# A causal mask moved from TensorE products to a GpSimd select in a gated linear attention layer followed by a quantised MLP

## The chip, the core and the metric

The kernel runs on one core of a Trainium2 chip. TensorE (PE) multiplies matrices and writes its sums to eight PSUM banks; VectorE (DVE), ScalarE (ACT) and GpSimd (POOL) work on tiles in SBUF, the first two on PSUM as well; SyncE (SP) issues nearly all DMAs. Each engine has its own queue and takes its instructions in order; semaphores tie the queues together. The metric is the device time of one execution in microseconds (us), lower is better.

## What is computed

The input x is 4 batches of 512 tokens with 512 features. The first layer is gated linear attention with 4 heads of 128 features over chunks of 128 tokens (4 chunks per batch, 16 in all), the second an MLP whose weights come as four-bit codes with scales.

```python
x = x + attention(layernorm(x))          # y only; the other outputs are dropped
x = x + ffn(layernorm(x))                # NVFP4 weights, 512 -> 4096 (gate, up) -> 512

# attention, per batch b, chunk n, head h
k     = k / max(norm(k), 1e-12)
cla   = cumsum(log(sigmoid(za) + 1e-6))            # within the chunk
decay = where(causal, exp(cla_i - cla_j), 0)       # 128 x 128, lower triangle
attn  = (q @ k.T) * beta_j * decay
y     = attn @ v + (q @ state) * exp(cla_i)
kw    = k * beta * exp(cla_end - cla)
state = state * exp(cla_end) + v.T @ kw
```

The mask `where(causal, ...)` is the part that the change is about.

## The kernel before

**Order of the work.** One schedule is written out by hand (`tc.manual_schedule()`, L811): the order in the code is the order in every queue. A loop over positions p (L856 to L900, then L901) lays a block of TensorE products first and then calls `behind(p)` (L656), which lays the attention work of a chunk behind it. For the first batches a block is `product_v`, `product_q` or `product_k` (four each per batch, L398, L422, L436); near the end of batch 3 the blocks become those of the MLP (`mlp`, L780, with `gate_up` L707 and `down` L745). Chunk (b,n), the chunk n of batch b, takes three positions in a row:

- p % 3 == 0, the lead: `chunk_lead` (L543) transposes k; `take_roots` (L344) runs the square roots of the norms that are waiting; `chunk_decay` (L553) makes the decays.
- p % 3 == 1, the scores: `settle` finishes the norms (among them `brn` and `kwf`, the per-row factors of v and k, L454 to L461, kept in `ss`); `chunk_scores` (L590) makes q·k, kw and vb and multiplies the scores by the decays.
- p % 3 == 2, the sums: `turn` (L358) transposes the normed rows; `chunk_sums` (L615) makes dp (the state's addend) and yp (the output), adds yp to x and starts the second layer's norm.

The factors of a chunk with n = 2 or 3 are usually settled a chunk earlier; those of n = 0 and 1 are settled in the chunk's own scores position. In batch 3, where the k products stand apart, (3,2) is settled in its own scores position too.

**The decays and the mask.** `gates_sums` (L513) makes row sums of the log gates: `rps` (L520) on 48 partitions, of which 0 to 15 hold one row per chunk and head rounded down a little and 32 to 47 the remainder (`pieces`, L521 to L526), and spreads them over the heads' columns (`rowsum`, L527). `all_of` (L159, L178) holds per chunk n a selector, 48 x 128, with ones in the rows of that chunk. In `chunk_decay` the product of selector and rowsum gives every row the cumulative sums of all heads: once as `pc` (L558, only for n > 0), whose exponential `cd` scales q (`qc`, two GpSimd products, L568), and once more as `pm` (L560), onto which a second product (L561) of the identity with `negm` adds -32768 where j > i. Four exponentials (L577), one per head with bias `ncla`, turn pm into `dm`; the -32768 makes the masked entries zero. GpSimd then scales the old state (L585), and in `chunk_scores` makes kw (L607, not for n = 3) and vb (L611). VectorE multiplies dm by the scores (L612).

**GpSimd's queue** for a chunk with n > 0 thus reads qc, qc, state, kw, vb. Without DMAs of its own it holds nothing else but the memset of `la` (L498).

**Buffers.** `Homes` (L94) hands out 42 tiles of 2 KB per partition (`one_k`) and 24 of 4 KB (`two_k`), the longest free first. PSUM tiles go round the eight banks in order.

**Around the change.** The MLP goes over the batches in rounds. The second layer's normed rows are split into three parts, written to HBM (`h<-g`, L388) and read back for each round (`x<-h`, L310); the first MLP round of batch 3 can begin only when (3,3) has been through all of this. Weights are unpacked by VectorE and ScalarE in small steps (`unpack`, L292) between the other work.

Of the kernel before, what the change touches and what calls it, by code (L numbers as in the profile page):

```python
# [21 lines left out]
P = 128  # L22
# [13 lines left out]
def f32(t):  # L36
    return t.bitcast(F32)
# [3 lines left out]
def tile_gated_linear_attention__then__nvfp4_geglu(  # L41
# [90 lines left out]

    ident = const.tile([P, P], F32, tag="ident", name="ident")
    make_identity(nc, ident)
    ident_r = const.tile([P, P], F32R, tag="ident_r", name="ident_r")

    tri = const.tile([P, P], F32, tag="tri", name="tri")
    nc.gpsimd.memset(tri, 1.0)
# [1 line left out]
        out=tri, in_=tri, compare_op=ALU.is_ge, fill=0.0, base=0,  # L140
        pattern=[[1, P]], channel_multiplier=-1,
    )

    home = one_k.get("neg")
    neg = heads(f32(home))
    nc.gpsimd.memset(neg, 0.0)
    nc.gpsimd.affine_select(
        out=neg, in_=neg, compare_op=ALU.is_ge, fill=-32768.0, base=0,
        pattern=[[0, H], [1, P]], channel_multiplier=-1,
    )  # L150
    negm = const.tile([P, H, P], F32R, tag="negm", name="negm")
    ones = const.tile([P, P], F32, tag="ones", name="ones")
    nc.gpsimd.memset(ones, 1.0)


    R2 = 32 + NCH * H
    one_of_h = const.tile([R2, H], F32, tag="one_of_h", name="one_of_h")
    of_n = const.tile([R2, 2, NCH], F32, tag="of_n", name="of_n")
    all_of = const.tile([R2, NCH, P], F32R, tag="all_of", name="all_of")  # L159
    eps_ln = const.tile([P, 1], F32, tag="eps_ln", name="eps_ln")  # L160
    nc.gpsimd.memset(eps_ln, 1e-5)
    eps_la = const.tile([P, 1], F32, tag="eps_la", name="eps_la")
    nc.gpsimd.memset(eps_la, 1e-6)

    def constants():
        nc.vector.tensor_copy(ident_r, ident)
        nc.vector.tensor_copy(negm, neg)
        one_k.put(home)
        nc.vector.tensor_reduce(
            one_of_h, ident[:R2, :R2].rearrange("p (n h) -> p h n", h=H), AX.X, ALU.add  # L170
        )
        for i in range(2):
            nc.vector.tensor_reduce(
                of_n[:, i, :],
                ident[:R2, 32 * i : 32 * i + NCH * H].rearrange("p (n h) -> p n h", h=H), AX.X, ALU.add,
            )
        nc.vector.tensor_tensor(of_n[:, 0, :], of_n[:, 0, :], of_n[:, 1, :], ALU.add)
        nc.vector.tensor_copy(all_of, of_n[:, 0, :].unsqueeze(2).to_broadcast([R2, NCH, P]))  # L178


    def dequant(pk, sc, n, w3, key):
# [306 lines left out]
    def gates_ln(b):  # L488


        ea, u = gt["ea"], gt["u"]
        alpha, w1, dd, eq, lw = (gate(b, nm) for nm in ("alpha", "w1", "dd", "eq", "lw"))
        nc.vector.tensor_scalar(ea, ea, 1.0, None, ALU.add)
        nc.vector.reciprocal(alpha, ea)
        nc.vector.tensor_scalar(w1, u, 1.0, None, ALU.add)

        la = gate(b, "la", R2)
        nc.gpsimd.memset(la, 0.0)  # L498
        nc.scalar.activation(la[:, :NG], alpha, AF.Ln, bias=eps_la)
# [5 lines left out]
        nc.vector.tensor_copy(la[:, 32:], la[:, :NG])  # L505
        nc.vector.tensor_tensor(lw, lw, dd, ALU.mult)
        nc.vector.tensor_tensor(lw, lw, eq, ALU.add)
        nc.vector.tensor_tensor(lw, lw, u, ALU.mult)
        beta[b] = gate(b, "beta")
        zb = zs[b][:, :, H:]  # L510
        nc.vector.scalar_tensor_tensor(th(beta[b]), zb, 0.0, th(lw), ALU.max, ALU.add)

    def gates_sums(b):  # L513
        la = gt["la"]
        cps = psum(f"cps{b}")
        nc.tensor.matmul(cps[:, :NG], tri, la[:, :NG], start=True, stop=True)
        nc.tensor.matmul(cps[:, NG : 2 * NG], ones, la[:, :NG], start=True, stop=True)

        rps = psum(f"rps{b}")
        nc.tensor.matmul(rps[:R2, :P], la, tri, start=True, stop=True)  # L520
        pieces = gate_pool.tile([R2, P], F32R, tag="pieces", name=f"pieces{b}")  # L521
        nc.scalar.activation(pieces, rps[:R2, :P], AF.Copy, scale=HI)
        ncla[b], bdte[b], td[b] = (gate(b, nm) for nm in ("ncla", "bdte", "td"))
        nc.vector.tensor_scalar(ncla[b], cps[:, :NG], -1.0, None, ALU.mult)
        nc.vector.tensor_tensor(bdte[b], cps[:, NG : 2 * NG], ncla[b], ALU.add)
        nc.vector.tensor_tensor(pieces[32:], rps[32:R2, :P], f32(pieces)[32:], ALU.subtract)  # L526
        rowsum[b] = one_k.get(f"rowsum{b}")  # L527
        nc.vector.tensor_tensor(
            heads(rowsum[b][:R2, :]), f32(pieces).unsqueeze(1).to_broadcast([R2, H, P]),
            one_of_h.unsqueeze(2).to_broadcast([R2, H, P]), ALU.mult,  # L530
        )
# [21 lines left out]
    def chunk_decay(b, n):  # L553

        toks = slice(n * P, (n + 1) * P)
        pc = psum(f"pc_{b}_{n}") if n > 0 else None
        if n > 0:
            nc.tensor.matmul(pc, all_of[:, n, :], rowsum[b][:R2, :], start=True, stop=True)  # L558
        pm = psum(f"pm_{b}_{n}")
        nc.tensor.matmul(pm, all_of[:, n, :], rowsum[b][:R2, :], start=True, stop=False)  # L560
        nc.tensor.matmul(pm, ident_r, negm.rearrange("p h c -> p (h c)"), start=False, stop=True)  # L561
        if n == NCH - 1:
            one_k.put(rowsum[b])
        if n > 0:
            cd, qc = one_k.get(f"cd_{b}_{n}"), one_k.get(f"qc_{b}_{n}")
            nc.scalar.activation(f32(cd), pc, AF.Exp)
            for c in range(H // 2):
                nc.gpsimd.tensor_tensor(  # L568
                    heads(f32(qc))[:, 2 * c : 2 * c + 2, :], f32(q_sb[b][c])[:, :, toks],
                    heads(f32(cd))[:, 2 * c : 2 * c + 2, :], ALU.mult,  # L570
                )
            one_k.put(cd)
            ch["qc"] = qc

        dm = one_k.get(f"dm_{b}_{n}")
        for h in range(H):
            nc.scalar.activation(  # L577
                f32(dm)[:, h * P : (h + 1) * P], pm[:, h * P : (h + 1) * P], AF.Exp,
                bias=ncla[b][:, n * H + h : n * H + h + 1],
            )  # L580
        ch["dm"] = dm
        if n + 1 < NCH:
            new = one_k.get(f"state_{b}_{n}")
# [4 lines left out]
            ch["new"] = new  # L588

    def chunk_scores(b, n):  # L590
        toks = slice(n * P, (n + 1) * P)
        sp = psum(f"sp_{b}_{n}")
        kT = ch.pop("kT")
        for h in range(H):
            nc.tensor.matmul(  # L595
                sp[:, h * P : (h + 1) * P], f32(kT)[:, h * P : (h + 1) * P],
                f32(q_sb[b][h // 2])[:, h % 2, toks], start=True, stop=True,
            )
        one_k.put(kT)
        if n == NCH - 1:  # L600
            two_k.put(*q_sb[b])
        dm = ch["dm"]
        brn, kwf = ss.pop((b, n))
        kt = k_sb.pop((b, n))
        if n + 1 < NCH:
            kw = one_k.get(f"kw_{b}_{n}")
            nc.gpsimd.tensor_tensor(heads(f32(kw)), heads(f32(kt)), bc(kwf), ALU.mult)  # L607
            ch["kw"] = kw
        one_k.put(kt)
        vb = one_k.get(f"vb_{b}_{n}")  # L610
        nc.gpsimd.tensor_tensor(heads(f32(vb)), heads(f32(v_sb[b, n])), bc(brn), ALU.mult)  # L611
        nc.vector.tensor_tensor(f32(dm), sp, f32(dm), ALU.mult)  # L612
        ch["vb"] = vb

    def chunk_sums(b, n):  # L615
        v = v_sb.pop((b, n))
# [39 lines left out]
    def behind(p):  # L656
# [295 lines left out]
```

## Time and profile before

| | |
|---|---|
| time, median of 3 runs | 1349.43 us |
| the three runs | 1351.72, 1349.36, 1349.43 us |
| the profiled execution | 1351.12 us, of which 1349.4 us are the span |
| mean granted TensorE clock | 0.992 |
| stretch 188 to 198 us of the profile | granted clock at 0.50 from about 192.4 to 195.8 us |
| other stretches at 0.50 | about 274.3 to 281.1 us and from 342.6 us for about 3 us |
| DMA | 238.67 MB, 177 GB/s on average |

The profile is of one execution. Busy time is a union over the span; "idle before" in a group is the time in which the engine waited just before these instructions, with the instruction that ended most of the wait. TensorE's products overlap, so the mean duration of one is longer than the distance between two starts; where a distance is meant, starts are compared. A granted clock of 0.50 means that TensorE was let run at half its speed. POOL's spans are rough.

### The profile page before, as it was taken

Reading aid. Unit: us, or ns where it says so; the run is one execution under the profiler, and the core shown is the slowest. Engines: PE = TensorE matmul, PEld = TensorE weight load, DVE = VectorE, ACT = ScalarE, POOL = GpSimd, SP = SyncE. Lnnn points to the kernel's source line nnn. Section 1 sums busy time; section 2 is a strip of 40 time slices with the busy share of each in tenths; the row PEclk is TensorE's granted clock in tenths of the full one; section 3 lists DMA queues with packets and bytes.
Section 4 is the critical chain, followed back from the end, with each engine's and each line's share of the span. In section 5 each row is a group of like instructions: output and inputs, shape, how many; then the busy total and the mean of one; then the engine's idle time right before and its main releaser. Section 6 shows DMA issues by size and latency. Waiting matters only on the chain.

```text
span 1349.4 us, 17021 instructions
## 1 busy us (share of the span) xinstructions
PE 1319.6 (98%) x5828; PEld 1047.7 (78%) x5828; DVE 989.2 (73%) x1639; ACT 488.3 (36%) x855; POOL 62.0 (5%) x78
## 2 busy tenths in 40 slices
PE   8999999979999999999999999999999999999997
PEld 5576767657788888888888888888888888888885
DVE  4576766588677777777777777777778787777656
ACT  2554545535333333333333333333333333333322
POOL 0031313110000000000000000000000000000000
PEclk9999999989999999999999999999999999999998
DMA  7033334875656565656565656565656565554446
GB/s 234 24 101 103 103 94 122 285 220 180 239 172 188 171 194 176 192 180 196 179 199 182 198 183 195 192 194 179 192 171 213 172 205 175 184 172 156 156 172 234
DMA packets 174950, 238.67 MB, mean 177 GB/s; under 512 B 15888, under 2 KB 74256, under 8 KB 174864
## 3 DMA queue, kind: packets, MB, share of 16 engines
q1 hardware_dynamic: 174160, 237.30, 54.4%
q8 instruction: 46, 0.75, 0.2%
q10 hardware_dynamic: 704, 0.28, 0.1%
q14 instruction: 40, 0.33, 0.1%
HBM read 184.05 MB, written 53.48 MB: 176 GB/s over the span
## 4 chain that ended last, share of the span: by engine, by line
PE 89%; DVE 4%; ACT 3%; DMA 2%; issue 1%; POOL 1%; SPq 0%; ACTq 0%; DVEq 0%; POOLq 0%
PE pa L716 33%; PE p_d L754 25%; PE pb L716 17%; PE pq L428 4%; PE pva L403 2%; PE pvb L410 2%; PE pk L440 1%; DMA x<-h 1%; PE yp L637 1%; PE dp L624 1%; PE sp L595 1%; PE yp L639 1%; ACT dm L577 0%; ACT L349 0%; DMA x<-in_x 0%
## 5 line engine op out<-in xcount | busy, mean ns | idle before, releaser
L716 PE MATMUL pa<-x,wgu 128*128 128x512 f32 x2048 | 509.2, 390 | 0.8 <-DMA x<-h 0.7
L716 PEld LDWEIGHTS pa<-x,wgu 128*128 128x128 f32 x2048 | 384.9, 188 | 82.1 <-DMA x<-h 2.4
L754 PE MATMUL p_d<-wd,i 128*128 128x512 f32 x1536 | 358.5, 391 | 7.4 <-ACT i L737 2.9
L754 PEld LDWEIGHTS p_d<-wd,i 128*128 128x128 f32 x1536 | 288.6, 188 | 71.7 <-ACT i L737 3.9
L722 ACT ACTIVATE t<-pb 128x512 f32<-128x512 f32 x256 | 151.2, 591 | 354.0 <-PE pb L716 351.0
L716 PE MATMUL pb<-x,wgu 128*128 128x512 f32 x1024 | 275.0, 390 | 0.6 <-DMA x<-h 0.4
L723 DVE TENSOR_TENSOR t<-pa,t 128x512 f32<-128x512 f32 x256 | 176.5, 690 | 102.3 <-ACT t L722 96.7
L716 PEld LDWEIGHTS pb<-x,wgu 128*128 128x128 f32 x1024 | 192.3, 188 | 41.7 <-DMA x<-h 1.3
L766 DVE SCALAR_TENSOR_TENSOR acc<-p_d,acc 128x512 f32<-128x512 f32 x140 | 96.0, 686 | 109.6 <-PE p_d L754 106.4
L737 ACT ACTIVATE i<-t 128x512 fp32r<-128x512 f32 x128 | 81.0, 633 | 194.7 <-DVE t L734 191.7
L727 ACT ACTIVATE t<-t 128x512 f32<-128x512 f32 x128 | 81.1, 633 | 154.7 <-DVE t L723 154.7
L767 DVE TENSOR_TENSOR acc<-acc,p_d 128x512 f32<-128x512 f32 x140 | 96.4, 688 | 14.6
L739 DVE TENSOR_TENSOR i<-t,i 128x512 fp32r<-128x512 f32 x128 | 88.1, 689 | 24.5 <-ACT i L737 23.0
L734 DVE SCALAR_TENSOR_TENSOR t<-t,t 128x512 f32<-128x512 f32 x128 | 88.6, 692 | 4.4
L740 DVE SCALAR_TENSOR_TENSOR i<-i,t 128x512 fp32r<-128x512 f32 x128 | 87.6, 685 | 0.0
L440 PE MATMUL pk<-wk,hT 128*128 128x512 f32 x128 | 57.6, 592 | 0.0
L428 PE MATMUL pq<-hT,wq 128*128 128x512 f32 x128 | 57.5, 593 | 0.0
L428 PEld LDWEIGHTS pq<-hT,wq 128*128 128x128 f32 x128 | 23.7, 190 | 23.9 <-issue 23.4
L440 PEld LDWEIGHTS pk<-wk,hT 128*128 128x128 f32 x128 | 23.5, 190 | 23.6 <-issue 23.4
L211 DVE SCALAR_TENSOR_TENSOR wgu<-wgu,w_gu 128x1024 fp32r<-128x1024 f32 x32 | 39.4, 1233 | 2.4 <-ACT wgu L208 2.4
L202 DVE SCALAR_TENSOR_TENSOR w_gu<-i_gu,sc_gu 128x1024 f32<-128x1024 f16 x32 | 39.7, 1240 | 0.0
L214 DVE TENSOR_TENSOR wgu<-wgu,wgu 128x1024 fp32r<-128x1024 f32 x32 | 39.5, 1234 | 0.0
(133 smaller groups left out, 914.1 us busy)
## 6 DMA issues: line engine op xcount, KB each, us to landing
x<-h SPq DMA_DIRECT2D x420, 256.0 KB
acc<-acc SPq DMA_DIRECT2D x264, 256.0 KB
h<-g SPq DMA_DIRECT2D x48, 256.0 KB
x<-in_x SPq DMA_DIRECT2D x16, 256.0 KB
pk_gu<-in_gate_p SPq DMA_DIRECT2D x32, 128.0 KB
sc_gu<-in_gate_s SPq DMA_DIRECT2D x64, 64.0 KB
pk_gu<-in_up_p SPq DMA_DIRECT2D x32, 128.0 KB
sc_gu<-in_up_s SPq DMA_DIRECT2D x64, 64.0 KB
```

The lines of the kernel that those rows point to most:

```text
L428: nc.tensor.matmul(pq, f32(wq[k // 2])[:, k % 2, h * P : (h + 1) * P], f32(hT[b][k // 2])[:, k % 2, :], start=(k == 0), stop=(k == KC - 1),)
L440: nc.tensor.matmul(pk, f32(hT[b][k // 2])[:, k % 2, n * P : (n + 1) * P], f32(wk[k // 2])[:, k % 2, :], start=(k == 0), stop=(k == KC - 1),)
L716: nc.tensor.matmul(o, w3[j][:, k % 2, c * P : (c + 1) * P], x[j * KC + k], start=(j == js[0] and k == 0), stop=(j == js[-1] and k == KC - 1),)
L722: nc.scalar.activation(f32(t), pb, AF.Copy, scale=-1.0 / ONE_E)
L723: nc.vector.tensor_tensor(f32(t), pa, f32(t), ALU.add)
L727: nc.scalar.activation(f32(g), f32(g), AF.Gelu_apprx_tanh, scale=ONE_E)
L734: nc.vector.scalar_tensor_tensor(f32(u), f32(g), ONE_E, f32(u), ALU.mult, ALU.mult)
L739: nc.vector.tensor_tensor(il, f32(u), f32(ih), ALU.subtract)
L740: nc.vector.scalar_tensor_tensor(im, f32(ih), ONE_E, f32(u), ALU.mult, ALU.subtract)
L754: nc.tensor.matmul(o, inter[i][j][:, n * P : (n + 1) * P], wd[ms[i] // 2][j][:, ms[i] % 2, :], start=(i == 0 and j == js[0]), stop=(i == L ...
L766: nc.vector.scalar_tensor_tensor(a, pas[2 * n], ONE_E, a, ALU.mult, ALU.add)
L767: nc.vector.tensor_tensor(a, a, pas[2 * n + 1], ALU.subtract)
```

## The change

The mask is no longer added by a product. `neg`, `negm` and `ident_r` go, with the memset, the select and the two casts that made them. There is one product per chunk, `pc`, for all n; the exponentials of dm read it, and a GpSimd `affine_select` on the 128 x 512 tile then sets the entries with j > i to zero in place. It stands in GpSimd's queue behind qc and ahead of the state's scaling, and VectorE's product of dm with the scores waits for it.

The selector `all_of`, `la`, `rps`, `pieces` and `rowsum` go from 48 to 128 partitions; the added rows are zero.

The part of `chunk_scores` that makes kw and vb becomes `chunk_values`. It is called at the lead as well, behind `chunk_lead` and ahead of `take_roots` and `chunk_decay`; where the chunk's factors are settled by then (n = 2 and 3, but not (3,2)), kw and vb are made there, ahead of qc, and the call in `chunk_scores` does nothing.

```diff
-    ident_r = const.tile([P, P], F32R, tag="ident_r", name="ident_r")
...
-    home = one_k.get("neg")
-    neg = heads(f32(home))
-    nc.gpsimd.memset(neg, 0.0)
-    nc.gpsimd.affine_select(
-        out=neg, in_=neg, compare_op=ALU.is_ge, fill=-32768.0, base=0,
-        pattern=[[0, H], [1, P]], channel_multiplier=-1,
-    )
-    negm = const.tile([P, H, P], F32R, tag="negm", name="negm")
...
-    R2 = 32 + NCH * H
-    one_of_h = const.tile([R2, H], F32, tag="one_of_h", name="one_of_h")
-    of_n = const.tile([R2, 2, NCH], F32, tag="of_n", name="of_n")
-    all_of = const.tile([R2, NCH, P], F32R, tag="all_of", name="all_of")
+    one_of_h = const.tile([P, H], F32, tag="one_of_h", name="one_of_h")
+    of_n = const.tile([P, 2, NCH], F32, tag="of_n", name="of_n")
+    all_of = const.tile([P, NCH, P], F32R, tag="all_of", name="all_of")
...
-        nc.vector.tensor_copy(ident_r, ident)
-        nc.vector.tensor_copy(negm, neg)
-        one_k.put(home)
...
-        la = gate(b, "la", R2)
+        la = gate(b, "la", P)
         nc.gpsimd.memset(la, 0.0)
...
-        nc.tensor.matmul(rps[:R2, :P], la, tri, start=True, stop=True)
-        pieces = gate_pool.tile([R2, P], F32R, tag="pieces", name=f"pieces{b}")
-        nc.scalar.activation(pieces, rps[:R2, :P], AF.Copy, scale=HI)
+        nc.tensor.matmul(rps[:, :P], la, tri, start=True, stop=True)
+        pieces = gate_pool.tile([P, P], F32R, tag="pieces", name=f"pieces{b}")
+        nc.scalar.activation(pieces, rps[:, :P], AF.Copy, scale=HI)
...
     def chunk_decay(b, n):
...
-        pc = psum(f"pc_{b}_{n}") if n > 0 else None
-        if n > 0:
-            nc.tensor.matmul(pc, all_of[:, n, :], rowsum[b][:R2, :], start=True, stop=True)
-        pm = psum(f"pm_{b}_{n}")
-        nc.tensor.matmul(pm, all_of[:, n, :], rowsum[b][:R2, :], start=True, stop=False)
-        nc.tensor.matmul(pm, ident_r, negm.rearrange("p h c -> p (h c)"), start=False, stop=True)
+        pc = psum(f"pc_{b}_{n}")
+        nc.tensor.matmul(pc, all_of[:, n, :], rowsum[b], start=True, stop=True)
...
             nc.scalar.activation(
-                f32(dm)[:, h * P : (h + 1) * P], pm[:, h * P : (h + 1) * P], AF.Exp,
+                f32(dm)[:, h * P : (h + 1) * P], pc[:, h * P : (h + 1) * P], AF.Exp,
                 bias=ncla[b][:, n * H + h : n * H + h + 1],
             )
+        nc.gpsimd.affine_select(
+            out=heads(f32(dm)), in_=heads(f32(dm)), compare_op=ALU.is_ge, fill=0.0, base=0,
+            pattern=[[0, H], [1, P]], channel_multiplier=-1,
+        )
         ch["dm"] = dm
...
-    def chunk_scores(b, n):
...
+    def chunk_values(b, n):
+
+        if (b, n) not in ss:
+            return
         brn, kwf = ss.pop((b, n))
         kt = k_sb.pop((b, n))
         if n + 1 < NCH:
...
         one_k.put(kt)
         vb = one_k.get(f"vb_{b}_{n}")
         nc.gpsimd.tensor_tensor(heads(f32(vb)), heads(f32(v_sb[b, n])), bc(brn), ALU.mult)
+        ch["vb"] = vb
+
+    def chunk_scores(b, n):
...
+        chunk_values(b, n)
+        dm = ch["dm"]
         nc.vector.tensor_tensor(f32(dm), sp, f32(dm), ALU.mult)
-        ch["vb"] = vb
...
             if chunk:
                 chunk_lead(cb, n)
+                chunk_values(cb, n)
             take_roots()
```

More of the change, by code (lines that the diff above doesn't have):

```diff
@@ L165, in constants @@
     def constants():
-        nc.vector.tensor_copy(ident_r, ident)
-        nc.vector.tensor_copy(negm, neg)
-        one_k.put(home)
         nc.vector.tensor_reduce(
-            one_of_h, ident[:R2, :R2].rearrange("p (n h) -> p h n", h=H), AX.X, ALU.add
+            one_of_h, ident.rearrange("p (n h) -> p h n", h=H), AX.X, ALU.add
         )
@@ L174, in constants @@
                 of_n[:, i, :],
-                ident[:R2, 32 * i : 32 * i + NCH * H].rearrange("p (n h) -> p n h", h=H), AX.X, ALU.add,
+                ident[:, 32 * i : 32 * i + NCH * H].rearrange("p (n h) -> p n h", h=H), AX.X, ALU.add,
             )
         nc.vector.tensor_tensor(of_n[:, 0, :], of_n[:, 0, :], of_n[:, 1, :], ALU.add)
-        nc.vector.tensor_copy(all_of, of_n[:, 0, :].unsqueeze(2).to_broadcast([R2, NCH, P]))
+        nc.vector.tensor_copy(all_of, of_n[:, 0, :].unsqueeze(2).to_broadcast([P, NCH, P]))
     def dequant(pk, sc, n, w3, key):
@@ L504, in gates_ln @@
         nc.vector.reciprocal(dd, dd)
-        nc.vector.tensor_copy(la[:, 32:], la[:, :NG])
+        nc.vector.tensor_copy(la[:, 32 : 32 + NG], la[:, :NG])
         nc.vector.tensor_tensor(lw, lw, dd, ALU.mult)
@@ L525, in gates_sums @@
         nc.vector.tensor_tensor(bdte[b], cps[:, NG : 2 * NG], ncla[b], ALU.add)
-        nc.vector.tensor_tensor(pieces[32:], rps[32:R2, :P], f32(pieces)[32:], ALU.subtract)
+        nc.vector.tensor_tensor(pieces[32:64], rps[32:64, :P], f32(pieces)[32:64], ALU.subtract)
         rowsum[b] = one_k.get(f"rowsum{b}")
         nc.vector.tensor_tensor(
-            heads(rowsum[b][:R2, :]), f32(pieces).unsqueeze(1).to_broadcast([R2, H, P]),
-            one_of_h.unsqueeze(2).to_broadcast([R2, H, P]), ALU.mult,
+            heads(rowsum[b]), f32(pieces).unsqueeze(1).to_broadcast([P, H, P]),
+            one_of_h.unsqueeze(2).to_broadcast([P, H, P]), ALU.mult,
         )
@@ L588, in chunk_decay @@
             ch["new"] = new
+    def chunk_values(b, n):
+        if (b, n) not in ss:
+            return
+        brn, kwf = ss.pop((b, n))
+        kt = k_sb.pop((b, n))
+        if n + 1 < NCH:
+            kw = one_k.get(f"kw_{b}_{n}")
+            nc.gpsimd.tensor_tensor(heads(f32(kw)), heads(f32(kt)), bc(kwf), ALU.mult)
+            ch["kw"] = kw
+        one_k.put(kt)
+        vb = one_k.get(f"vb_{b}_{n}")
+        nc.gpsimd.tensor_tensor(heads(f32(vb)), heads(f32(v_sb[b, n])), bc(brn), ALU.mult)
+        ch["vb"] = vb
     def chunk_scores(b, n):
@@ L601, in chunk_scores @@
             two_k.put(*q_sb[b])
+        chunk_values(b, n)
         dm = ch["dm"]
[L603 to L611, printed above, removed]
         nc.vector.tensor_tensor(f32(dm), sp, f32(dm), ALU.mult)
-        ch["vb"] = vb
     def chunk_sums(b, n):
```

## The prediction

> **What bounds the kernel now.** I read the page first, then busy time by stretches, then TensorE's instructions in order of time, then the chain that ended last. I call the chunk of batch b and index n "(b,n)"; times are from the start of the profiled span.
>
> ```profile
> PE 1319.6 (98%) x5828; PEld 1047.7 (78%) x5828; DVE 989.2 (73%) x1639; ACT 488.3 (36%) x855; POOL 62.0 (5%) x78
> ...
> 350.00:400.00 50.00, 50.00 (x222) 41.39 (x221) 41.07 (x60) 19.49 (x32) 0.00 (x0) 1.00 0.56 180
> ```
>
> TensorE is busy 98% of the span, and the stretch from 350 to 400 us (columns: length, busy time of PE, PEld, DVE, ACT, POOL, granted clock, DMA) shows the MLP as pure TensorE: 222 products in 50.00 us, 0.225 us each. The change touches nothing there. It touches the sixteen chunks, which run from 47 to 316 us, so the question is how much sooner the MLP is let go.
>
> The chain says what lets it go:
>
> ```profile
> 294.76 1.01 POOL kw L607
> 295.82 1.16 PE dp L624 x8
> ...
> 329.45 2.33 DMA h<-g
> ...
> 337.56 5.28 DMA x<-h
> ...
> 342.88 0.79 PE pb L716
> ```
>
> From about 246 us (the k product of (3,1) handed over) to 343 us the chain runs through ScalarE, VectorE, GpSimd and at last through batch 3's h written to HBM and read back. TensorE is on it only for MLP products and for dp and yp, never for the mask products. So **a TensorE saving counts up to 246 us and is lost behind it**.
>
> **The change, part by part.**
>
> *Selector and mask products.* TensorE in order of time, chunk (0,1) and two groups of transposes:
>
> ```profile
> 63.37 0.60 PE L547 MATMUL tpk<-ident,k 128*128 128x128 f32 x4
> 63.90 0.50 PE L558 MATMUL pc<-rowsum,all_of 48*128 48x512 f32 x1
> 64.24 0.39 PE L560 MATMUL pm<-rowsum,all_of 48*128 48x512 f32 x1
> 64.56 0.50 PE L561 MATMUL pm<-negm,ident_r 128*128 128x512 f32 x1
> 64.90 1.94 PE L403 MATMUL pva<-wva,hT 128*128 128x264 f32 x8
> ...
> 72.81 0.60 PE L362 MATMUL tp_f<-ident,hn_f 128*128 128x128 f32 x4
> 73.24 0.60 PE L362 MATMUL tp_a<-ident,hn_a 128*128 128x128 f32 x4
> ```
>
> Ends are modelled, so I take start to start. From tpk to pva is 1.53 us. Four transposes take 0.43 (72.81 to 73.24), so pc, pm, pm and the switches around them take 1.10. With n = 0 (47.21 to 48.51) it is 1.30. Afterwards one product on 128 rows is left. [...] The rows show 0.32 to 0.34 us a product next to a 48-row operand, against 0.225 in the MLP, all on 128 rows. I take the rows: a chunk falls to 0.43 + 0.23 = 0.67, saving 0.86 with n > 0 and 0.63 with n = 0: 12 x 0.86 + 4 x 0.63 = 12.8 us. The rps product on 128 columns ends the same kind of switch: cps to the next product was 0.79 (35.58 to 36.37), an estimate for after is 0.58: 0.2 per batch. Wider la, pieces and rowsum cost nothing: elements per partition stay, but for the memset of la (0.13 us, nothing queued behind it on GpSimd). The casts of ident and neg at the start (0.22 and 0.42 us) lie ahead of a wait of VectorE for x of 1.52 us: nothing, and a gain without that cover.
>
> *How much of 12.8 us lies on the path.* Behind 246 us 0.63 + 3 x 0.86 = 3.2 us are lost. Before it, chunk by chunk, with the select at its only row:
>
> ```profile
> L147 POOL TENSOR_SCALAR_AFFINE_SELECT neg<-neg 128x512 f32<-128x512 f32 x1 | 0.6, 637 | 0.0
> ...
> 72.21 1.22 POOL L611 TENSOR_TENSOR vb<-v,brn 128x512 f32<-128x512 f32 x1
> ...
> 101.45 1.63 POOL L568 TENSOR_TENSOR qc<-q,cd 128x256 f32<-128x256 f32 x2 [11.05 <-ACT cd L566]
> ...
> 106.33 0.69 DVE L446 TENSOR_TENSOR k<-pk,bk 128x512 f32<-128x512 f32 x1 [1.09 <-PE pk L440]
> ```
>
> n = 1: GpSimd runs qc, select, state, kw, vb with no pause; the exponentials are done (69.6) before qc is (70.0). The select pushes vb's end from 73.43 to 74.03, and yp, which started at 74.57, starts at 74.09: gain 0.48, not 0.86. The same in (1,1) and (2,1) gives 0.41 and 0.35. n = 2: kw and vb are done a slot earlier, behind them qc, select and state; dp and yp don't wait. The product of sp with dm on VectorE waits for the select, 1.0 us later in (0,2); queued behind it is the scaling of w_gu, then g, which had 2.1 us of idle. Gain 0.86 each, 2.58. Without the early kw and vb, vb would end at 90.9 where TensorE asks for it at 90.0. The two issue no DMA; they move from 87.3 to about 74.1, behind vb of (0,1), beside VectorE's fields of i_gu and g. What they hold up there has room: VectorE's statistics end at 79.7 and ScalarE takes the root at 82.4. Without that room, up to 1 us each. They hold one buffer more for a slot. n = 3: qc ends 103.08, select 103.68, dm by 104.4, then bdte (0.2) and wgu (1.2): VectorE comes to k at 105.75, where TensorE would have let it at 105.3. From k on VectorE and ScalarE set the time through (1,0), so the gain is 106.33 - 105.75 = 0.58; in (1,3) 0.54; in (2,3), with more idle time on VectorE, all of 0.86 + 0.2. n = 0 of batches 0 to 2: TensorE already waits for kw there; 0. Batch 0's rps: 0.2.
>
> Sum: 1.24 + 2.58 + 2.18 + 0.2 = **6.2 us**.
>
> *On the chain behind 246 us.* The select enters it at (3,2), between qc and state: there the norms of k come too late for an early kw, so kw moves from 294.7 to 295.3 and dp to 296.4. It costs nothing at full clock: p_d behind yp runs 6 products (to 299.97) and then waits until 300.99 for g. In (3,3) vb leaves the place beside w_gu (1.42 against 1.22 us): -0.2. In (3,0) the select waits for the exponentials (251.89) ahead of kw and vb; vb then ends at 254.6, about where yp started (254.7). In (3,1) VectorE's hn_f took 1.38 instead of 0.55 us beside kw; what stands there shifts by 0.6, worth -0.8 to +0.2; I take 0.
>
> *The clock.* What TensorE no longer spends it waits, in front of n = 0 and (3,2).
>
> ```profile
> 188.95:192.37 3.42, 1.75 (x13) 1.36 (x12) 2.73 (x4) 0.71 (x2) 2.98 (x2) 1.00 0.00 0
> 192.40:195.80 3.40, 3.40 (x13) 2.88 (x12) 3.33 (x7) 0.91 (x3) 0.00 (x0) 0.50 0.56 158
> ```
>
> In (2,0) 3.42 us with TensorE busy about half were followed by 3.4 us at granted clock 0.50: 1.7 us lost. [...] The row shows that half-idle is enough, so I charge it. Idle time in (1,0) grows from about 1.7 to 2.9 us in five, in (3,2) from 2.3 to 3.8 in a row. Estimates: (1,0) 0.6 x 1.3 = 0.8 us; (3,2) 0.7 beyond its slack; (2,0) 0.9 x 1.6 = 1.45 us where the run before had no such window.
>
> **The sum.** The profiled execution took 1351.12 us, 1349.4 of them span; two of the three timed runs took 1349.4, 1.7 less, what the window in (2,0) cost the profile. Against the profile: 1351.12 - 6.2 - 0.2 + 0.8 + 0.7 = 1346.2. Against the median, with (2,0) charged: 1349.43 - 6.4 + 2.95 = **1346.0**, which I take.
>
> The select's cost d in the loop is the unknown. Below: 0.6, its row, and no less, since the same 512 elements are read and written. Above: 2.0, what kw (1.04 alone) took beside VectorE's w_gu in (0,2). I take 0.6, since it reads one tensor. Each 0.1 costs about 0.5 us (two places in each of batches 0 and 1, one in batch 2).
>
> **Rivals.** (A) The clock never drops: 1349.43 - 6.4 = 1343.0. [...] Against: 192.4 us. (B) The gain is mostly eaten: d near 1.2 (-3 us) or every stall window at half clock, 1347 to 1350. For it: four of the 28 kw and vb took 2.0 instead of 1.04. (C) Slower: the select is blocked or slow each time. With d = 2.0 it costs 7 us over the sum and another 1.0 in (3,2), where it passes the 1.0 us of slack: 1346.0 + 8.0 = 1354.0. It decides from d = 1.3 on (no gain at all). For it: select and VectorE meet in the same stretches. Against: its row and its one input. (D) Padding gains nothing, and the switch stays: then only 0.33 x 2 instead of 0.86 a chunk; n = 2 and (2,3) lose 0.2 each: 1346.8.
>
> **Chances.** Forecast 0.40, A 0.15, B and D 0.29, C 0.16. A measurement of this kernel tells 0.2% (2.7 us) from no change. Faster by that (below 1346.7): the forecast nearly whole, A, a little of B and D: 0.56. Within: 0.27. Slower (over 1352.1): C and a stall I don't see, 0.17. The range reaches below A, where part of the n = 1 waits (1.3 us in all) would not come, to 1342.2, and up to between B and C, 1351.0.
>
> **What would show it.** Right: tpk to the next product 0.67 us; selects at 0.6; k behind (0,3) after 9.6 us from its tpk (10.2 before); kw and vb of n = 2 ahead of qc; first x product of batch 3 some 3 to 6 us sooner. Wrong: selects over 1.2 us; pc still at 0.33; new windows at clock 0.5 in (0,0) or (3,3); VectorE idle on GpSimd ahead of dm for more than 1 us.

## The result, and the profile after

The changed kernel takes **1348.72 us** (median of 20 runs, 1346.42 to 1350.45), the kernel before beside it 1350.73 us (20 runs, 1349.36 to 1352.37). The ratio is 0.9983 with a 95% interval of 0.9976 to 0.9989: 2.0 us faster, which is less than the 0.2% that was set as the bound of "no change". The median shown of before, 1349.43 us, came from three runs and was 1.3 us below that of 20. The profiled execution of after took 1346.61 us (span 1344.9).

First the page (busy time by engine), then the same MLP stretch as before, from the changed kernel:

```profile
PE 1309.6 (97%) x5800; PEld 1044.3 (78%) x5800; DVE 987.4 (73%) x1637; ACT 488.4 (36%) x855; POOL 72.0 (5%) x92
```

```profile
350.00:400.00 50.00, 50.00 (x222) 41.41 (x221) 37.73 (x55) 16.57 (x27) 0.00 (x0) 1.00 0.49 156
```

28 products are gone and TensorE's busy time fell by 10.0 us; the MLP is what it was, 222 products in 50.00 us. GpSimd's busy time rose by 10.0 us. TensorE in order of time at chunk (0,1):

```profile
62.54 0.60 PE L533 MATMUL tpk<-ident,k 128*128 128x128 f32 x4
62.90 0.48 PE L543 MATMUL pc<-rowsum,all_of 128*128 128x512 f32 x1
63.21 1.94 PE L389 MATMUL pva<-wva,hT 128*128 128x264 f32 x8
```

From tpk to pva it is 0.67 us, to the digit what was predicted, instead of 1.53. GpSimd in order of time, chunks (0,1) and (0,2) of the changed kernel:

```profile
67.83 1.41 POOL L550 TENSOR_TENSOR qc<-q,cd 128x256 f32<-128x256 f32 x2 [9.85 <-ACT cd L548]
69.20 0.82 POOL L563 TENSOR_SCALAR_AFFINE_SELECT dm<-dm 128x512 f32<-128x512 f32 x1
69.99 1.20 POOL L571 TENSOR_TENSOR state<-state,td 128x512 f32<-128x512 f32 x1
71.16 1.04 POOL L584 TENSOR_TENSOR kw<-k,kwf 128x512 f32<-128x512 f32 x1
72.16 1.22 POOL L588 TENSOR_TENSOR vb<-v,brn 128x512 f32<-128x512 f32 x1
73.33 1.22 POOL L584 TENSOR_TENSOR kw<-k,kwf 128x512 f32<-128x512 f32 x1
74.52 1.03 POOL L588 TENSOR_TENSOR vb<-v,brn 128x512 f32<-128x512 f32 x1
83.83 1.41 POOL L550 TENSOR_TENSOR qc<-q,cd 128x256 f32<-128x256 f32 x2 [8.28 <-ACT cd L548]
85.19 0.64 POOL L563 TENSOR_SCALAR_AFFINE_SELECT dm<-dm 128x512 f32<-128x512 f32 x1
```

The kw and vb of (0,2) run at 73.33 and 74.52, ahead of its qc. The select takes 0.64 us in nearly all chunks, but 0.82 to 0.84 in the chunks with n = 1 of batches 0 to 2; in (0,1) VectorE makes hn_f (68.76 to 69.5 us) and hn_a (from 69.63) beside it. What waits for GpSimd is in the profile's list of waits (waiter, what it waited for, sum, count, longest):

```profile
PE dp L616 <- POOL kw L584: 7.1, 7, 3.4
...
PE p_d L747 <- DVE dm L605: 3.0, 1, 3.0
```

Ahead of dp the waits grew from 4.4 to 7.1 us, ahead of p_d from 2.1 to 3.0: TensorE now waits where it worked. The granted clock in (3,1), first before, then after (columns: length, busy time of PE, PEld, DVE, ACT, POOL, granted clock, DMA):

```profile
260.00:285.00 25.00, 18.71 (x83) 13.93 (x82) 18.61 (x34) 10.16 (x17) 4.65 (x5) 0.86 0.52 160
```

```profile
260.00:285.00 25.00, 18.04 (x83) 14.57 (x82) 21.19 (x40) 8.93 (x16) 4.57 (x6) 0.80 0.54 178
285.00:300.00 15.00, 11.57 (x60) 10.02 (x59) 10.10 (x17) 6.19 (x12) 6.45 (x7) 0.89 0.66 211
```

The stretch at half clock in (3,1) lasts 6.8 us before (274.29 to 281.12) and 10.2 us after (265.86 to 276.10); (3,2), at full clock before, has one of 3.4 us (289.75 to 293.17).

**Where the time went, by position.** The table shows how much sooner than before TensorE reaches a point in the profiled execution of after. Two differences between the two executions are not the change's. After is 0.60 us ahead when the log gates are summed, at 35 us: full clock was first granted at 9.86 us in it and at 11.46 us in before; up to there the products of v start 0.44 us apart, behind it 0.22. And before lost 1.67 us in (2,0) to a half-clock stretch that after has not. The last column leaves both out.

| point | sooner by | of it the change |
|---|---|---|
| tpk (0,0) | 0.82 us | 0.22 us |
| tpk (1,0) | 2.79 | 2.19 |
| tpk (2,0) | 4.47 | 3.87 |
| tpk (3,0), 238 us | 7.74 | 5.47 |
| tpk (3,2) | 6.09 | 3.82 |
| yp (3,2) | 4.65 | 2.38 |
| yp (3,3), 309 us | 5.56 | 3.29 |
| end of span | 4.5 | 2.2 |

The first 0.22 us are batch 0's row sums: from the first product of cps to tpk of (0,0) it is 11.63 us with 48 rows (before) and 11.41 with 128 (after). So 5.47 us are won ahead of (3,0), and 3.2 of them are given back behind it.

**The clock run by run.** Each run reports the mean granted clock of its whole span. Over the kernel before (the 63 runs beside the experiments, medians 1350.7 to 1351.2 from one comparison to the next) 0.001 less clock goes with 0.80 us more time; over after's 20 runs with 0.64 us. The median clock is 0.992 before and 0.989 after. At an equal 0.992 the runs average 1350.9 us (32 runs of before) and 1347.3 us (3 of after), 3.6 us apart; at 0.991 and 0.993, with two runs of after each, it is 5.2 and 3.2. **The change is worth some 3.6 us at equal clock, and brings on a lower clock that takes back some 2 us** (0.003 by 0.64 to 0.80 us per 0.001). The mean is a rough measure, since not every stretch at half clock costs time: the one from 1334.23 to 1341.06 us in after is 3.4 us longer than before's at that place, and after's lead is the same 4.52 us ahead of it (1326.17 against 1330.69 us) and at the last addition of VectorE (1341.23 against 1345.75).

### The profile page after: what moved, and what is told of

Same layout as the page of the kernel before. It is cut to its first block, busy times and chain, and to the rows that moved or that the text cites. A ratio compares the mean times of both kernels' runs of the same rounds, so it can differ in the third digit from the quotient of the medians.

```text
span 1344.9 us, 16986 instructions
## 1 busy us (share of the span) xinstructions
PE 1309.6 (97%) x5800; PEld 1044.3 (78%) x5800; DVE 987.4 (73%) x1637; ACT 488.4 (36%) x855; POOL 72.0 (5%) x92
## 4 chain that ended last, share of the span: by engine, by line
PE 82%; DVE 5%; issue 5%; ACT 4%; POOL 2%; DMA 2%; SPq 1%; POOLq 0%; DVEq 0%; ACTq 0%
PE pa L709 33%; PE p_d L747 25%; PE pb L709 16%; PE pq L414 3%; PE pva L389 1%; DMA x<-h 1%; PE pvb L396 1%; PE pk L426 1%; PE dp L616 1%; ACT L335 1%; ACT dm L559 1%; DMA x<-in_x 1%; PE yp L629 1%; POOL kw L584 0%; POOL vb L588 0%
```

## The experiments

Each is timed beside the kernel before on the same chip. e1 to e4, e5 to e8 and e9 to e11 ran on three chips, where before took 1351.2, 1350.66 and 1350.92 us, so a difference between two of these groups, or to after, can be off by some 0.5 us.

| kernel | median, us | lowest to highest | clock, median | ratio to before, 95% |
|---|---|---|---|---|
| before (the runs beside e1 to e4) | 1351.2 | 1349.4 to 1353.05 | 0.992 | |
| after | 1348.72 | 1346.42 to 1350.45 | 0.989 | 0.9976 to 0.9989 |
| e1 no select | 1343.96 | 1343.17 to 1347.54 | 0.991 | 0.9940 to 0.9965 |
| e2 fill | 1346.87 | 1346.42 to 1348.06 | 0.992 | 0.9960 to 0.9982 |
| e3 not early | 1352.43 | 1351.54 to 1354.0 | 0.989 | 1.0005 to 1.0021 |
| e4 rows 48 | 1349.81 | 1346.68 to 1351.49 | 0.990 | 0.9979 to 0.9997 |
| e5 state late | 1345.25 | 1343.27 to 1347.34 | 0.988 | 0.9947 to 0.9972 |
| e6 late fill | 1342.92 | 1342.74 to 1343.28 | 0.993 | 0.9930 to 0.9955 |
| e7 before, fill | 1351.27 | 1350.47 to 1352.91 | 0.993 | 0.9997 to 1.0013 |
| e8 rows only | 1347.28 | 1345.7 to 1348.67 | 0.991 | 0.9963 to 0.9982 |
| e9 rows, fill | 1347.88 | 1346.62 to 1348.58 | 0.992 | 0.9968 to 0.9987 |
| e10 x fill | 1341.78 | 1340.82 to 1342.55 | 0.994 | 0.9921 to 0.9946 |
| e11 products late | 1345.57 | 1344.13 to 1345.98 | 0.990 | 0.9961 to 0.9975 |

### e1: what the select costs

```diff
-        nc.gpsimd.affine_select(
-            out=heads(f32(dm)), in_=heads(f32(dm)), compare_op=ALU.is_ge, fill=0.0, base=0,
-            pattern=[[0, H], [1, P]], channel_multiplier=-1,
-        )
```

> The changed kernel without its select; the causal mask is left out, so the decays above the diagonal stay in. Median of the changed kernel 1348.7 us, of the kernel before 1350.7. Queue theory (the select's 0.6 to 0.8 us stand in GpSimd's queue ahead of kw and vb for n = 1 and (3,2), and ahead of VectorE's dm for n = 3): 0.3 to 0.7 us for each n = 1, 0.1 for n = 3, 0.6 in (3,2): 1346 to 1347. Clock theory (what is given back goes to windows at half clock while TensorE waits in front of n = 0, (3,1) and (3,2), which come with or without a select): 1348 to 1349.

Measured 1343.96 us, 4.8 less than after; the mask is left out of this kernel. That is more than either theory gave. The clock's median is 0.991 instead of 0.989, worth some 1.4 us; at an equal 0.991 the runs average 1343.5 (three) against 1346.8 us (two of after), 3.2 us for the select itself. The prediction's own rate, 0.5 us for each 0.1 us of d, gives 3.0 for d = 0.6. Since the mask is left out, the numbers that the later products work on differ too.

### e2: unread products in the waits

```diff
+            for _ in range(4 if n == 0 else 12 if (b, n) == (B - 1, 2) else 0):
+                nc.tensor.matmul(dp, all_of[:, n, :], rowsum[b], start=True, stop=True)
...
+        for _ in range(3 if n == 0 else 0):
+            nc.tensor.matmul(yp, all_of[:, n, :], rowsum[b], start=True, stop=True)
```

They stand ahead of dp and of yp in `chunk_sums`; the next product overwrites them.

> The changed kernel with selector products that nobody reads put where TensorE waits: 4 ahead of dp and 3 ahead of yp for n = 0, 12 ahead of dp in (3,2), 0.225 us each. Clock theory: half-speed windows in front of (1,0), (2,0) and (3,2) go, the median falls to where the best runs of the changed kernel lie, 1346.4, with less spread, and granted clock 0.992 or more in each run. Queue theory: the waits end when kw and vb are made, not sooner, so 1348.7, or some tenths more where a product that nobody reads is still running when kw is done.

1346.87 us: more work on TensorE, and 1.9 us less time than after. The six runs lie within 1.7 us where after's 20 spread over 4.0, and the median clock is back at 0.992. Part of the fill sticks out of its waits (0.6 us at (0,0), 0.9 at (3,0)).

### e3: kw and vb where they were

```diff
                 chunk_lead(cb, n)
-                chunk_values(cb, n)
```

> The changed kernel with kw and vb of all chunks made at the scores, behind qc, select and state. As worked out in the prediction, vb of n = 2 then ends about 0.9 us after TensorE asks for it in each of batches 0 to 2, and n = 3 has vb behind the select, early enough: 1348.7 + 2.0 to 2.7 = 1350.7 to 1351.4. Rival (early kw and vb are hidden anyway, since VectorE and ScalarE set the time from n = 3 on): 1348.7.

1352.43 us, 3.7 more than after where 2.0 to 2.7 were expected, and the only kernel here whose interval lies above before. In its profile n = 2 has nothing left: from the yp of (0,1) to that of (0,2) TensorE loses 0.15 us on before where after gains 0.76. In (1,0) a stretch at half clock appeared from 122 to 126 us. The early kw and vb belong to the select: without them the rest of the change makes the kernel slower.

### e4: 48 rows with the select

```diff
+    R2 = 32 + NCH * H
-    all_of = const.tile([P, NCH, P], F32R, tag="all_of", name="all_of")
+    all_of = const.tile([R2, NCH, P], F32R, tag="all_of", name="all_of")
```

The same for la, rps, pieces and rowsum.

> The changed kernel with the selector, pieces and rowsum on 48 partitions as before; all else as changed. If a product beside a 48-row operand costs a switch (0.33 us and about 0.1 at its sides against 0.225): tpk to the next product about 0.87 instead of 0.67 us, 0.2 us for each of n = 2 and for (2,3) and for each batch's rps, 1349.5 to 1350. [...]

1349.81 us, 1.1 more than after, as expected, but beside the runs' spread (their intervals overlap) the time decides nothing. The profile does. TensorE of e4 at (0,1):

```profile
62.86 0.60 PE L534 MATMUL tpk<-ident,k 128*128 128x128 f32 x4
63.39 0.50 PE L544 MATMUL pc<-rowsum,all_of 48*128 48x512 f32 x1
63.82 2.05 PE L390 MATMUL pva<-wva,hT 128*128 128x264 f32 x8
```

From tpk to pva 0.96 us against 0.67 with 128 rows: one product costs 0.29 us more because its operands have 48 rows between operands of 128.

### e5: the state scaled behind kw and vb

```diff
-                nc.gpsimd.tensor_tensor(
-                    heads(f32(new)), heads(f32(state[b])), bc(td[b][:, n * H : (n + 1) * H]), ALU.mult
-                )
+                old = state[b]
+                def scale():
+                    nc.gpsimd.tensor_tensor(
+                        heads(f32(new)), heads(f32(old)), bc(td[b][:, n * H : (n + 1) * H]), ALU.mult
+                    )
+                if (b, n) in k_sb:
+                    ch["scale"] = scale
+                else:
+                    scale()
...
         chunk_values(b, n)
+        if "scale" in ch:
+            ch.pop("scale")()
```

> The changed kernel with one instruction moved: where kw and vb are made in the scores position (n = 1, and (3,1), (3,2)), GpSimd scales the old state behind kw and vb, not ahead of them. kw and vb then end about 1.0 us sooner there. Queue theory (GpSimd's queue qc, select, state, kw, vb is what n = 1 and (3,2) wait for): yp of n = 1 comes 0.5 to 0.9 us sooner in each of three batches, the wait ahead of dp in (3,2) falls from 3.4 us to about 2.4, together 1345.5 to 1347 against 1348.7. Rival (what n = 1 gains is waited for again at the following n = 0, or lost to more time at granted clock 0.50): 1348 to 1349.

1345.25 us, 3.5 less than after, a little below the range of the queue theory. By position n = 1 gains over after 0.55, 0.65 and 0.89 us in the three batches; dp of (3,2) starts 5.4 us sooner than after's, start-ups set equal (4.93 by the clock of the two profiles, and e5 began 0.42 later); 2.1 of it are those of n = 1. One instruction out of the way of kw and vb was enough. GpSimd in (3,2), first after, then e5:

```profile
286.25 1.41 POOL L550 TENSOR_TENSOR qc<-q,cd 128x256 f32<-128x256 f32 x2 [21.14 <-ACT cd L548]
287.61 0.64 POOL L563 TENSOR_SCALAR_AFFINE_SELECT dm<-dm 128x512 f32<-128x512 f32 x1
288.21 1.04 POOL L571 TENSOR_TENSOR state<-state,td 128x512 f32<-128x512 f32 x1
289.21 1.04 POOL L584 TENSOR_TENSOR kw<-k,kwf 128x512 f32<-128x512 f32 x1
```

```profile
282.32 1.42 POOL L550 TENSOR_TENSOR qc<-q,cd 128x256 f32<-128x256 f32 x2 [17.84 <-DMA x<-h]
283.69 0.64 POOL L563 TENSOR_SCALAR_AFFINE_SELECT dm<-dm 128x512 f32<-128x512 f32 x1
284.29 1.04 POOL L592 TENSOR_TENSOR kw<-k,kwf 128x512 f32<-128x512 f32 x1
```

From qc to kw 2.96 us in after, 1.97 in e5. Yet e5's median clock is 0.988, and its runs spread over 4 us: the lower clock takes part of what the queue gives.

### e6 and e7: filling only the waits, with and without the change

```diff
+            for _ in range(4 if n == 0 and b in (1, 2) else 9 if (b, n) == (B - 1, 2) else 0):
+                nc.tensor.matmul(dp, all_of[:, n, :], rowsum[b], start=True, stop=True)
...
+        for _ in range(2 if n == 0 and b in (1, 2) else 0):
+            nc.tensor.matmul(yp, all_of[:, n, :], rowsum[b], start=True, stop=True)
```

> The kernel of e5 with products that nothing reads laid into TensorE's waits: four ahead of dp and two ahead of yp in (1,0) and (2,0), nine ahead of dp in (3,2), 21 in all (4.7 us at 0.225 us each if none lay in a wait). Clock theory (about 0.85 us of time per stretch of 3.4 us at granted clock 0.50, and idle time ahead of it brings it on): about two such stretches fewer than in e5, and 1344 to 1345.5. Rival (the stretches don't depend on these waits): 1346.5 or more, by as much as the products stick out of the waits.

> The kernel before with the same unread products in its waits, on its own 48-row operands: four ahead of dp and two ahead of yp in (1,0) and (2,0), five ahead of dp in (3,2). It tells whether filling is worth the same without the change. Clock theory: 1349.4 to 1350.3 against 1351.2, since its waits are shorter and it has 6.3 half-clock stretches a run against 8.7. Rival (the waits don't matter): 1351.2 to 1352.

e6 takes 1342.92 us, 2.3 less than e5 and less than was expected, all five runs within 0.54 us, at a median clock of 0.993. Its 21 added products are the only difference to e5. e7, the same fill in the kernel before (five products in (3,2)), takes 1351.27 against 1350.66 us, no gain: here the clock theory missed. Before's clock was at 0.992 already, and the fill brought it to 0.993. The fill pays where a change has made waits, not everywhere.

### e8 and e9: the rows alone

```diff
-    R2 = 32 + NCH * H
+    R2 = P
```

(la, rps and pieces follow; the remainder stays in rows 32 to 47.) e9 adds the products of e7 to it, seven in (3,2).

> The kernel before with one part of the change alone: selector, la, rps, pieces and rowsum on 128 rows; the mask stays two products, no select, kw and vb where they were. By the rows of the trace (0.33 us a product beside a 48-row operand, 0.225 between 128-row ones) tpk to the next product falls by about 0.35 us with n > 0 and 0.25 with n = 0; up to 246 us some 3 us of TensorE, of which n = 0 and part of n = 1 is waited out: 1348.5 to 1349.7 against 1351.2. [...]

> The kernel of e8 (before, with 128-row selector operands, mask by products) with the unread products of e7 in its waits, seven instead of five ahead of dp in (3,2). Against e6 it tells what the select is worth once the waits are filled on both sides. If the mask products still stand on the path up to 246 us in n = 2 and 3 (two products of 0.225 us per chunk, most of them not waited out), e6 stays ahead by 2 us or more: 1345 to 1346. Rival (the select only moves the wait from TensorE to GpSimd): within 1 us of e6, 1342.9 to 1344.

e8 takes 1347.28 us, 3.4 less than before, where 1.5 to 2.7 were expected. That is 1.4 less than the whole change, though the two intervals overlap. TensorE of e8 at (0,1), with all three products still there:

```profile
63.37 0.60 PE L547 MATMUL tpk<-ident,k 128*128 128x128 f32 x4
63.72 0.48 PE L558 MATMUL pc<-rowsum,all_of 128*128 128x512 f32 x1
64.04 0.40 PE L560 MATMUL pm<-rowsum,all_of 128*128 128x512 f32 x1
64.28 0.39 PE L561 MATMUL pm<-negm,ident_r 128*128 128x512 f32 x1
64.51 1.94 PE L403 MATMUL pva<-wva,hT 128*128 128x264 f32 x8
```

From tpk to pva 1.14 us instead of 1.53: the rows alone give 0.39 of the 0.86, with nothing added to any queue. e9, e8 with fills, gains nothing on e8 (1347.88) and lies outside both of its expectations. So the two halves of the change, measured as medians: rows with the product mask -3.4 us (e8); select and early kw and vb with 48 rows about -1.4 (e4 against its before); both together -2.0, no more than the rows alone. With its waits mended, though, the select side leads: e6 is 5.0 us ahead of e9. Part of that is not the select's, since e6 also has the early kw and vb and the later state, which e9 has not.

### e10: the clock where the change is not

```diff
+                        for _ in range(2 if i == 0 and key == "3_0" and (0, 2) <= (j, k) < (2, 0) else 0):
+                            nc.tensor.matmul(
+                                pb, all_of[:, 0, :], all_of.rearrange("p n c -> p (n c)"), start=True, stop=True
+                            )
```

> The kernel of e6 with twelve more unread products, two ahead of each of the third to eighth first products that read x of batch 3, where TensorE takes a product every 0.66 us as its x arrives (328 to 331.4 us), about a third busy, and was granted 0.50 from 331.5 to 339 us. No part of the change touches this place. Clock theory (a stretch in which TensorE idles about half or more is followed by half clock): the two half-clock stretches there go, 1.5 to 3 us: 1340 to 1341.5. Rival (the clock drops for another reason, say load of the whole chip, or the x transfers set the pace to 339 us anyway): 1342.9, or 0.3 us more.

Stretches of e6, then of e10, same columns as above:

```profile
328.00:331.40 3.40, 2.48 (x5) 0.92 (x5) 1.82 (x3) 0.00 (x0) 0.00 (x0) 1.00 0.93 324
331.50:335.00 3.50, 3.13 (x6) 1.78 (x7) 0.00 (x0) 0.27 (x1) 0.00 (x0) 0.54 1.05 403
335.00:339.00 4.00, 4.00 (x12) 3.17 (x11) 1.82 (x2) 0.96 (x2) 0.00 (x0) 0.55 1.06 388
```

```profile
328.00:331.40 3.40, 3.40 (x16) 2.77 (x15) 3.09 (x6) 0.00 (x0) 0.00 (x0) 1.00 0.95 345
331.50:335.00 3.50, 2.38 (x9) 1.24 (x7) 0.12 (x1) 0.00 (x0) 0.00 (x0) 1.00 0.98 342
335.00:339.00 4.00, 3.77 (x15) 2.90 (x16) 1.82 (x2) 1.23 (x2) 0.00 (x0) 1.00 1.05 405
```

The half-clock stretches are gone, and 1.1 us with them (1341.78 us); all five runs have a mean clock of 0.994 or 0.995, those of e6 0.991 or 0.993. Nothing but twelve products in TensorE's idle time was added, so the drop after time that is idle in part is shown here by itself. (The 2.48 us of the first row count the products' modelled ends; at 0.225 us each, e6's five products are 1.1 us of 3.4.) That the gain is smaller than expected fits the DMA share of 0.95 to 1.05: x arrives at its own pace, and at full clock TensorE waits for it (busy 2.38 of 3.50 us from 331.5 us on). e10 is the fastest kernel here, 0.9934 of before (0.9921 to 0.9946), 6.9 us below after.

### e11: product masks in the last chunks

```diff
+        pm = pc
+        if b == B - 1 and n > 0:
+            pm = psum(f"pm_{b}_{n}")
+            nc.tensor.matmul(pm, all_of[:, n, :], rowsum[b], start=True, stop=False)
+            nc.tensor.matmul(pm, ident_r, negm.rearrange("p h c -> p (h c)"), start=False, stop=True)
...
+        if b < B - 1 or n == 0:
             nc.gpsimd.affine_select(
```

> The kernel of e6 with the mask of (3,1), (3,2) and (3,3) made by the two products again, on 128 rows, and no select there. Behind 246 us the prediction said that a TensorE saving is lost and that the select costs nothing. If the select on GpSimd does cost there (0.6 us each at (3,1) and (3,2), where kw waits behind it): 1341.5 to 1342.5. If it costs nothing and the two products are hidden: 1342.9. If the products are not hidden (six of 0.225 us): 1343.5 to 1344.3.

1345.57 us, 2.65 more than e6, outside all three. In the profiles, set equal at (3,0), e11 gains 0.11 us on e6 by the yp of (3,2) (the select is out of the way) and loses 0.66 by that of (3,3). The rest goes with the clock, 0.990 against 0.993; which stretch loses it is open, since the profile shows a run at 0.993.

## Why the prediction was right or wrong

The forecast was 1346.0 us; 1348.72 lies inside the range, but in the place of rival B, "gain mostly eaten", and on the "same" side that had 0.27. That it lies inside is owed to the width of the range (8.8 us), not to the sum. TensorE's own saving was right; what failed was the step that let the select and the waits behind 246 us cost almost nothing (0.5 us charged, 3.2 measured), and the start of the sum was low.

**TensorE's saving: right.** 0.86 us a chunk was predicted, from 1.53 to 0.67; the trace has 0.67, split otherwise: from tpk to pc 0.36 (0.43 was taken), from pc to pva 0.31 (0.23 was taken). The rows that the prediction took, 0.32 to 0.34 us a product against 0.225, held: by rival D, that padding gains nothing, e8 should have changed nothing; it gained 3.4 us. Rival D falls with it.

**The select's duration: nearly right.** 0.64 instead of 0.6, but 0.82 to 0.84 at n = 1, where it costs most. Rival C (d from 1.3 on) did not occur. That its one input is what kept the select short no run shows.

**"How much of 12.8 us lies on the path": 6.2 predicted, 5.47 measured.** From yp to yp: n = 1 gave 0.32, 0.20 and -0.03, 0.49 us instead of 1.24: the mis-sized part, the queue of qc, select, state, kw, vb sets it, as e5 shows by what it gains there, and the select in it took 0.2 us more than was put in. n = 2 gave 0.76 each, 2.28 instead of 2.58. n = 3 gave 0.89, 0.89, 0.88, 2.66 instead of 2.18, for VectorE reached k of (0,3) 9.39 us after tpk, not 9.6. Batch 0's row sums gave 0.22, as predicted. At the starts of (1,0) and (2,0) 0.2 were lost again. e3 confirms the early kw and vb: without them n = 2 loses the 0.9 us that the prediction worked out.

**"Costs nothing at full clock" behind 246 us: this step failed.** Charged was 0.7 - 0.2 us; 3.2 were given back. In (3,1) the select pushes state by 0.6 us; the prediction saw this shift and put it at 0, and didn't name the step of VectorE that goes with it. Here is that step (tensor_scalar on ss) with GpSimd's state, in before and in after, then e5, where state runs later:

```profile
268.38 1.04 POOL L585 TENSOR_TENSOR state<-state,td 128x512 f32<-128x512 f32 x1
268.50 0.69 DVE L450 TENSOR_REDUCE ss<-sq 128x4 f32<-128x512 f32 x1 [3.61 <-ACT sq L448]
269.22 0.22 DVE L452 TENSOR_SCALAR ss<-ss 128x4 f32<-128x4 f32 x1
...
269.90 1.38 DVE L334 TENSOR_SCALAR hn_f<-xr,mv_f,rs_f 128x512 f32<-128x512 f32 x1
```

```profile
260.82 0.69 DVE L436 TENSOR_REDUCE ss<-sq 128x4 f32<-128x512 f32 x1 [4.12 <-ACT sq L434]
261.31 1.04 POOL L571 TENSOR_TENSOR state<-state,td 128x512 f32<-128x512 f32 x1
261.54 0.83 DVE L438 TENSOR_SCALAR ss<-ss 128x4 f32<-128x4 f32 x1
...
262.83 1.38 DVE L320 TENSOR_SCALAR hn_f<-xr,mv_f,rs_f 128x512 f32<-128x512 f32 x1
```

```profile
258.86 0.69 DVE L436 TENSOR_REDUCE ss<-sq 128x4 f32<-128x512 f32 x1 [4.12 <-ACT sq L434]
259.58 0.17 DVE L438 TENSOR_SCALAR ss<-ss 128x4 f32<-128x4 f32 x1
...
260.21 1.39 DVE L320 TENSOR_SCALAR hn_f<-xr,mv_f,rs_f 128x512 f32<-128x512 f32 x1
```

An operation on 4 elements a row took 0.83 us beside state on GpSimd, and both end at about 262.4 us; apart from state it takes 0.17, and in before it started 0.2 us ahead of state's end and took 0.22. What makes the two end together no run here shows. But the prediction's own row of hn_f, 1.38 instead of 0.55 us beside kw, was already one of a VectorE operation that took longer beside GpSimd, and from it the step could have been looked for. It stands ahead of kwf and hn_f, so kw and, down VectorE's queue, TensorE's transposes (tp_f) are 0.6 us late: from L436 to hn_f it is 2.01 us in after, 1.40 in before, 1.41 in e1 and 1.35 in e5; from there on to tp_f 7.48 to 7.49 in all four.

Of the 3.2 us given back, the select is not the whole. In the profiles of before and after they divide so:

- (3,1): 1.65 us. 0.10 up to its tpk; 0.56 between tpk and dp, the step above; 0.99 between dp and tpk of (3,2), where after runs 4.9 us at half clock and before 2.8.
- (3,2): 1.44 us. The 0.84 that TensorE saves up to sp are waited away, since qc starts 7.2 us behind tpk in both; the select between qc and kw then costs 0.58; and from dp to yp it takes 1.86 us at half clock instead of 1.00.
- Up to yp of (3,3) 0.9 are won back.
- Behind it 1.07 are lost, 0.86 of them where the products read x of batch 3 (from 331.22 to 341.97 us in after, from 336.58 to 346.47 in before). Both have one 3.4 us stretch at half clock there, and TensorE waits for the transfers of x in between.

So the select's two places cost 1.15 us, the half clock some 1.8, and x 0.9. e1 has no select and still gives back 2.4 in its profile, from 10.0 us of lead at dp of (3,0) to 7.6 at the end, with the same two stretches as after (10.2 and 3.4 us). In after's slower runs, of which there is no profile, the shares can differ. "A TensorE saving counts up to 246 us and is lost behind it" holds for (3,2), but not everywhere: e11 has six products more behind 246 us and is 0.66 us later by (3,3), and e10 shows that a stretch at half clock still counts at 331 to 339 us.

**The clock: right in size, wrong in place.** Charged were 2.95 us against the median; 0.003 of clock costs about 2. That time which is idle in part is enough is borne out by e10: e6 has five products in the 3.4 us ahead of the drop there, e10 sixteen and no drop. But the stretches in (1,0) and (2,0) that 2.25 us of it stood for are not in after's profile, whose new ones are in (3,1) and (3,2). In the slower runs they may be there: e6 fills just the waits of (1,0), (2,0) and (3,2) and takes the median clock of e5 from 0.988 to 0.993. The one profile at 0.989, that of e3, has stretches in (1,0), at 122 us, and in (3,2), 6.8 us long from 293 us. No profile of such a run of after or e5 exists, so which of the three places loses most there stays open.

**The start of the sum.** The median of three runs was 1.3 us low. With 1350.73 the same working gives 1347.3, at the difference of -3.4 against -2.0 measured. At equal clock (0.992): -6.4 predicted, some -3.6 measured, and 0.7 of the difference is missing up to 238 us; the rest fell behind it.

**The signs named.** Right: 0.67 us, selects near 0.6, kw and vb of n = 2 ahead of qc, k of (0,3) sooner, the pb behind the last x of batch 3 at 337.5 us, 5.3 sooner than before. Of the wrong signs one came: VectorE idled 1.89 us on GpSimd ahead of dm in (0,3); but k behind it was early, so that sign was badly chosen. "pc still at 0.33" is nearly met by the 0.31 us from pc to pva, and misled as well, since the saving lies in the step ahead of pc. (0,0) and (3,3) have no half-clock stretch.

## What to carry to other kernels

The work moved here from a full engine to an idle one was paid for in that engine's queue, 3.2 us for the selects by e1 at equal clock: look for what stands ahead of the value that is waited for, and move first what nobody waits for. Here the state's scaling behind kw and vb was worth 3.5 us, more than the whole change had gained. When a saving turns into waits of TensorE, look at the granted clock of the stretches behind them, and at the spread of the runs; a wait with half clock behind it that can't be removed can be filled, as in e6 and e10 (2.3 and 1.1 us); in e7 and e9 filling gained nothing. And try a change's parts alone: wider operands, the part that put nothing into any queue, gave at least as much as the whole.

## What the runs showed of the hardware

- **Where half clock began.** In the profiles of before and after each of the ten stretches at granted clock 0.50 begins a whole number of times 3.413 us after full clock was first granted: in after, first at 9.86 us, those at 265.86, 289.75 and 337.54 us 75, 82 and 96 times; in before, first at 11.46 us, those at 192.37, 274.29 and 342.56 us 53, 77 and 97 times.
- **What stood ahead of it.** As an estimate, count each product at the distance of two starts in an unbroken row (0.225 us in the MLP, 0.43 for q and k, 0.22 for v, 0.11 on 128 columns), in steps of 3.413 us from the first full clock to 350 us. In the two profiles the six steps at full clock that were followed by half clock then hold 0.4 to 1.2 us of work, the 185 others 1.3 us or more. (2,0) held 1.20 us in before (188.96 to 192.37 us, half clock behind it) and 1.32 in after (183.94 to 187.35, none). In e6 five products in 3.4 us from 328 us were followed by half clock (0.54 and 0.55 in the next two rows), in e10 sixteen by full clock.
- **The clock as a price.** 0.001 of mean clock went with 0.64 to 0.80 us in the two kernels with 20 runs and more.
- **Operand rows.** A product with 48-row operands between products on 128 rows cost 0.29 us more than one padded with zero rows (0.96 against 0.67 us). The steps that make the operands took as long on 128 partitions as on 48: pieces 0.26 us in both, rowsum 0.69 and 0.68; the memset of la took 0.21 instead of 0.13 us.
- **GpSimd and VectorE together.** A select of 128 x 512 took 0.64 us in most chunks and 0.82 beside VectorE's hn_f in (0,1); a VectorE operation on 128 x 4 took 0.83 instead of 0.17 us beside GpSimd's scaling of the state.
